# Another load order, narrower first products and new ranks in a planned attention kernel

## The chip, the core and the metric

The kernel runs on one core of a Trainium2 chip. The metric is device microseconds from the start to the end of one execution. Before the change the median of three runs is 588.07 us (587.85 to 589.9). Engines are called as the profile calls them: PE multiplies, PEld loads its weights, DVE, ACT and POOL are the elementwise engines, SP issues DMAs.

## What is computed

Two cross attentions with 8 heads over x (2 x 2048 x 640), all in float32, and an output projection. The first attends from x to 124 text tokens. The second is an adapter over 4 more tokens, whose own queries attend to x before; its result has only 384 different rows, which are gathered to 2048 by fixed indices.

```python
query = hidden_states @ Wq
hs = _mha(query, enc @ Wk, enc @ Wv)                     # 8 heads of 80
ca_q1 = jnp.einsum('btc,th->bch', ca, Wq_ca)[:, indices, :]
ca_hs1 = _mha(ca_q1, residual, residual)                 # residual is x
ca_hs2 = _mha(ca_hs1 @ Wq, ca @ Wk_ca, ca @ Wv_ca)
out = (hs + ca_hs2) @ Wout + b_out + residual
```

## The kernel before

The order of all instructions is made while the program is built. Generators (`x_first`, `queries`, `text_scores`, `chain` and so on) yield pieces of work, `Do(engine, function, after, needs, ...)`, and the class `Desk` plays them against a model of the chip: each piece has a modelled length, each DMA a modelled landing, and every engine's list is written in the order in which the model runs it. On the chip every engine then keeps that order and waits on semaphores, whatever the real times are.

At each step `Desk.run` (L164) looks, engine by engine, for the earliest moment at which a piece could start, and takes among those that are ready then the one with the smallest sum of `order` (the rank given in the code plus an entry of the table `RANKS`, by the generator's name and how many of that name were begun before it) and `change` (L141). `change` is only counted for pieces that say in what shape they use PE's array: nothing in the shape of the moment, `LEAVE` when PE leaves the whole 128x128 array, `SWITCH` when it goes back to it, `ANOTHER` between two smaller shapes. Scores (`sc`, 64-row halves), hidden states (`ph`, 32-column quarters) and all products with Wq and Wout (`pq`, `po`, whole) carry a shape; the adapter's pieces (`s`, `acc`, `pyz`) carry none and have the lowest ranks.

```python
        if mode is None or mode == self.mode:
            return 0.0
        return self.LEAVE if self.mode == self.WHOLE else self.SWITCH if mode == self.WHOLE else self.ANOTHER
```

PE's other filler is `idle_work` (L564): 14 products of zeros (tile `unread`, two passes each), rank 9, that the planner puts wherever it sees PE with nothing else.

The start runs so. `first_loads` (L465) issues on SP: x's rows 0 to 127 and 128 to 255 (`x_rows`, 320 KB each), Wq in five chunks of its 640 rows (`chunk`, the fifth in `last`; the heads' 80 features are regrouped into chunks of 128), x's rows 256 to 511, then the small inputs, Wk_ca and Wk. `x_first` (L624) turns the first 512 rows of x so that features lie on partitions: for each 128 rows (k) DVE first collects the features that are not contiguous (`between`, tile `first_rows`, five copies), PE transposes chunk by chunk (tile `pt_x`), ACT or DVE copies the result into the tile `xt` and marks `("xpart", half, part)`. `queries` with `first=True` (L1160) multiplies by Wq over 256 rows at a time, the first half (k = 0, 1) chunk by chunk of the contraction as Wq lands, the second half later. A product over n rows in float32 is two passes of n columns on PE, for each of two banks and two output chunks.

After that come the keys and values, seven more blocks of 512 rows of x (`x_load`, `queries_fast`, by a scheme with fewer products), the adapter's maximum pass (`s`, reduced by DVE into `mx`), its exponentials (`s` to ACT's `ea`) and contraction (`acc`), for each of two batches, and for each 128 rows the scores, softmax (`m`, `p`, `eb`), a store and reload that turns the probabilities (`kept`, `pT`), the hidden states and the product with Wout, added to x by DVE (`x_more`, `last_rows`).

Of the kernel before, what the change touches and what calls it, by code (L numbers as in the profile page):

```python
# [14 lines left out]
P = 128  # L15
# [49 lines left out]
class Desk:  # L65
# [3 lines left out]
    ENGINES = ("PE", "ACT", "DVE", "POOL", "SP", "NONE")  # L69
    WHOLE, SWITCH, LEAVE, ANOTHER = (P, P), 157.7, 5.4, 131.2  # L70
    START = {(P, P): 0.107, (64, P): 0.143, (P, 64): 0.107, (64, 32): 0.1, (P, 32): 0.03}
# [13 lines left out]
    RANKS = {  # L85
        "adapter": {0: 3, 1: 5.5},
        "chain": {2: 9, 4: -18, 5: 11, 6: -3, 8: -1, 10: -8, 11: -0.6, 19: -3, 24: -3, 25: 8, 30: 11, 32: 8,
            34: -10, 35: -1, 36: -1.3, 39: 2, 41: 3.5, 42: 4, 45: 6, 48: -4, 49: -15, 52: -1, 53: 6, 58: 8,
            60: -6, 61: -6, 62: -9, 64: -1, 72: -3, 80: 2, 85: 3, 87: 7},
        "contract": {0: 5.5, 1: 6, 2: 6, 3: 8},  # L90
        "halves_away": {1: -13, 2: -2, 6: 7},
        "keys": {0: -11},
        "probabilities": {0: 6.1, 8: 9, 9: 6, 11: -7, 14: -3, 15: 4},
        "queries_fast": {0: 4, 4: -3},
        "rest_back": {1: 13, 4: 5, 9: 7, 10: 8},
        "second": {0: 6},
        "softmax": {0: 6, 2: -2, 4: -5, 8: 5, 10: 4, 11: -4, 14: -4, 16: 2, 17: 7, 21: 12, 22: 10, 25: 4},
        "sums_of_wq": {0: 9},
        "text_scores": {0: -3, 1: 9, 12: 5},
        "values_weights": {0: -17},  # L100
        "x_load": {1: 5.1, 4: 7, 5: 6},
        "y_rows": {2: 4, 3: 15, 5: -2},
        "yz_block": {2: 12, 3: -2, 6: 10, 7: 1.3},
    }
# [155 lines left out]
def kernel(  # L260
# [204 lines left out]
    def first_loads():  # L465
# [31 lines left out]
        for k in (0, 1):  # L497
            yield x_rows(k)
        for c in range(4):
            yield chunk(c)  # L500
# [123 lines left out]
    def x_first():  # L624
# [7 lines left out]
        for k in range(4):  # L632
# [4 lines left out]
            )), 1)  # L637
        for h in range(2):
            k0 = 2 * h
            for n, part in enumerate((  # L640
                [(k0, c) for c in range(4)], [(k0 + 1, c) for c in range(4)], [(k0, 4), (k0 + 1, 4)],
            )):

                def turn(s, part=part, n=n, k0=k0):
                    pt = early_bank(s[0], f"pt_x_{k0}_{n}")
                    for i, (k, c) in enumerate(part):
                        transpose(pt[:, i * P : (i + 1) * P], rows_by_chunk(rows_of[0][:, k], last[k], c), ident)
                    return pt

                op = yield Do("PE", turn, [("xlast", k0 + min(n, 1))], needs=[(early, 1)])  # L650
                to = xt[0, 0][0][:, k0 + n, :4] if n < 2 else xt[0, 0][0][:, k0 : k0 + 2, 4]
                src = op.value[:, : len(part) * P].rearrange("p (c s) -> p c s", s=P)
                yield Fork(one(Do(
                    EITHER, lambda to=to, src=src: copy(to, src), [op.at], frees=[(early, op.slots[0][0])],
                    marks=[("xpart", h, n)],
                )), 1)
        yield Do(
            "NONE", lambda: None, [("xpart", h, n) for h in range(2) for n in range(3)],
            frees=[(first_rows, at) for at in rooms] + [(staging, 0)], marks=[("x", 0, 0)],
# [500 lines left out]
    def queries(n, after, first=False):  # L1160
# [8 lines left out]
        if first:  # L1169
            yield Do("NONE", room, [], needs=[(qslots, 1)])  # L1170
            q = q_of[n][0]

            def product(to, h, i, c, start):
                matmul(
                    to, wq_of(i, c), t[:, 2 * h : 2 * h + 2, i, :], start=start, stop=(i == NCH - 1),
                    skip_group_check=True,
                )

            def two(pq, j, h, i):
                for m in range(2):  # L1180
                    product(pq[:, 2 * P * m : 2 * P * (m + 1)], h, i, 2 * j + m, i == 0 and m == 0)

# [8 lines left out]
            for i in range(NCH):  # L1191
                op = yield Do(
                    "PE", lambda i=i: [two(pq[j], j, 0, i) for j in range(2)],
                    [("wq", i)] + [("xpart", 0, k) for k in range(3 if i == NCH - 1 else 2)],
                )
            for j in range(2):
                yield kept(pq[j], j, 0, three[j], op.at)
            for h in range(2):
                for j in range(2 if h else 0):

                    def part(s, j=j):
                        to = bank(s[0], f"pq_{n}_{j}_1")
                        for i in range(2):
                            two(to, j, 1, i)
                        return to

                    op = yield Do("PE", part, after, needs=[(banks, 1)], mode=(P, P))
                    to, s = op.value, op.slots[0][0]
                    for i0, i1 in ((2, 4), (4, NCH)):
                        op = yield Do("PE", lambda i0=i0, i1=i1: [two(to, j, 1, i) for i in range(i0, i1)], mode=(P, P))  # L1210
                    yield kept(to, j, 1, s, op.at)
                for i0, i1 in ((0, 3), (3, NCH)):

                    def fifth(i0=i0, i1=i1, h=h):
                        for i in range(i0, i1):
                            product(pq[2][:, 2 * P * h : 2 * P * (h + 1)], h, i, 4, i == 0 and h == 0)

# [1154 lines left out]
```

## Time and profile before

| | before |
|---|---|
| median of three runs | 588.07 us (587.85 to 589.9) |
| the profiled execution, its time | 588.11 us |
| its span, first to last instruction | 586.4 us |
| PE busy | 578.6 us |
| DVE busy | 392.0 us |
| ACT busy | 313.2 us |
| granted TensorE clock | 0.999 |

The span is shorter than the time of the same execution by 1.7 us, which lie before the first and after the last instruction. In a timeline a row is one or several like instructions of one engine: start, length, engine, line, operation, tiles, shape, count, and in brackets how long the engine stood idle before it and what ended that. Matmuls overlap, so a row's length is longer than the distance to the next row's start; distances of starts are used where a price is wanted. Where a helper records each operation (L208, L218, L233, L253), the line says nothing and the tile's name tells what the instruction is for.

### The profile page before, as it was taken

The numbers are of one execution on the slowest core, as the hardware profiler recorded it, in microseconds if no ns is written. First come the engines' busy times: TensorE is split into PE (matmuls) and PEld (weight loads), VectorE is DVE, ScalarE is ACT, GpSimd is POOL, SyncE is SP. The second block draws the span as 40 slices with busy tenths as digits, with TensorE's granted clock in tenths as the row PEclk, the third lists the DMA queues.
The fourth block names the chain that finished last, engine by engine and source line by source line (L and its number), as shares of the span: only waits on it lengthen the run. The fifth ranks groups of instructions, "written<-read, shape, count | busy, mean of one in ns | idle before, by whom it ended". The sixth has DMA issues, their size and how long they took to land.

```text
span 586.4 us, 12250 instructions
## 1 busy us (share of the span) xinstructions
PE 578.6 (99%) x4681; PEld 374.8 (64%) x4681; DVE 392.0 (67%) x646; ACT 313.2 (53%) x881; POOL 141.7 (24%) x200
## 2 busy tenths in 40 slices
PE   9999999999999999999999999999999999999997
PEld 8786446676766566566576656655556566676675
DVE  2546899999999566356999999853255353544443
ACT  1413276686558789679847626368678612102200
POOL 9102112112205214010115225122041221322342
PEclk9999999999999999999999999999999999999999
DMA  8996876899566967324999959994658577699967
GB/s 254 231 215 116 204 105 180 173 212 182 148 198 149 219 144 193 114 75 155 246 264 260 235 150 206 295 265 122 154 124 248 128 198 201 142 261 267 264 162 195
DMA packets 153012, 112.27 MB, mean 191 GB/s; under 512 B 83701, under 2 KB 126581, under 8 KB 152954
## 3 DMA queue, kind: packets, MB, share of 16 engines
q1 hardware_dynamic: 147322, 100.80, 66.5%
q0 software_dynamic: 5632, 10.69, 10.5%
q8 instruction: 37, 0.61, 0.4%
q14 instruction: 21, 0.17, 0.1%
HBM read 71.23 MB, written 40.22 MB: 190 GB/s over the span
## 4 chain that ended last, share of the span: by engine, by line
PE 85%; DVE 9%; DMA 2%; issue 2%; ACT 2%; DVEq 0%
PE po L208 27%; PE pq L208 23%; PE acc L208 7%; PE ph L208 7%; PE sc L208 6%; PE s L208 6%; DVE mx L233 4%; PE pyz L208 2%; DVE eb L233 1%; PE pv L208 1%; PE pk L208 1%; DMA kept<-eb 1%; DMA zb<-z 1%; DVE m L233 1%; PE unread L208 1%
## 5 line engine op out<-in xcount | busy, mean ns | idle before, releaser
L233 DVE TENSOR_REDUCE mx<-s 128x4 f32<-128x2048 f32 x48 | 109.3, 2276 | 2.4 <-PE s L208 2.4
L233 ACT ACTIVATE ea<-s 128x2048 f32<-128x2048 f32 x48 | 91.0, 1895 | 30.8 <-PE s L208 30.6
L233 ACT ACTIVATE p<-sc,m 128x124 f32<-128x124 f32 x256 | 89.8, 383 | 7.5 <-DVE m L233 6.8
L208 PE MATMUL pq<-xt,wq_sb 128*128 128x256 f32 (+1 forms) x312 | 86.2, 416 | 0.1
L208 PE MATMUL po<-wout_sums,hs 128*128 128x320 f32 x256 | 78.9, 440 | 0.5 <-DVE x_more L233 0.5
L208 PE MATMUL po<-wout_sb,hs 128*128 128x320 f32 x248 | 76.6, 439 | 0.0
L233 DVE TENSOR_TENSOR x_more<-x_more,po 128x320 f32<-128x320 f32 x76 | 36.5, 484 | 52.3 <-PE po L208 51.8
L208 PEld LDWEIGHTS pq<-xt,wq_sb 128*128 128x128 f32 x312 | 56.8, 190 | 21.3 <-issue 13.7
L208 PEld LDWEIGHTS po<-wout_sums,hs 128*128 128x128 f32 x256 | 47.2, 190 | 23.6 <-issue 4.7
L208 PEld LDWEIGHTS po<-wout_sb,hs 128*128 128x128 f32 x248 | 45.6, 190 | 22.8 <-issue 4.2
L233 ACT ACTIVATION_READ_ACCUMULATOR p<-sc,m 128x1 f32 x256 | 57.9, 226 | 0.0
L2107 POOL DMA_INDIRECT x_more<-o,query x19 | 29.4, 1550 | 101.2 <-DVE x_more L233 86.5
L208 PE MATMUL acc<-ea,y_sb 128*32 128x384 f32 (+2 forms) x768 | 51.2, 385 | 0.0
L233 DVE TENSOR_REDUCE m<-sc 128x4 f32<-128x496 f32 x64 | 40.0, 662 | 11.2 <-PE sc L208 11.1
L233 DVE TENSOR_TENSOR last_rows<-last_rows,po 128x320 f32<-128x320 f32 x52 | 25.0, 485 | 31.6 <-PE po L208 31.2
L233 ACT COPY hs<-ph 128x512 f32<-128x512 f32 (+1 forms) x34 | 18.3, 545 | 51.7 <-PE ph L208 51.7
L208 PE MATMUL ph<-pT,vpad 128*32 128x256 f32 x768 | 45.0, 381 | 0.0
L233 ACT ACTIVATE p<-p,r 128x124 f32<-128x124 f32 x120 | 36.3, 387 | 10.9 <-DVE r L233 10.9
L233 POOL TENSOR_TENSOR p<-p,r 128x992 f32<-128x992 f32 x8 | 14.8, 1853 | 112.8 <-DVE r L233 112.8
L233 DVE STREAM_TRANSPOSE eb<-p 128x1024 f32<-128x1024 f32 x32 | 39.4, 1232 | 1.9 <-DMA kept<-eb 1.1
L208 PE MATMUL pq<-xt,wq 128*128 128x512 f32 (+1 forms) x90 | 40.1, 564 | 0.0
L208 PEld LDWEIGHTS sc<-kmain,q 64*128 64x128 f32 x512 | 31.5, 187 | 11.4 <-issue 6.1
(212 smaller groups left out, 814.7 us busy)
## 6 DMA issues: line engine op xcount, KB each, us to landing
kept<-eb SPq DMA_DIRECT2D x32, 512.0 KB, 4.4
pT<-kept SPq DMA_DIRECT2D x64, 256.0 KB, 6.7
landing<-away SPq DMA_DIRECT2D x60, 128.0 KB, 3.6
xi<-in_x_dram SPq DMA_DIRECT2D x56, 128.0 KB, 3.9
x_more<-in_x_dram SPq DMA_DIRECT2D x19, 320.0 KB, 6.6
out_dram<-x_more SPq DMA_DIRECT2D x18, 320.0 KB, 4.9
last_rows<-in_x_dram SPq DMA_DIRECT2D x13, 320.0 KB, 5.5
y<-yt SPq DMA_DIRECT2D x16, 256.0 KB, 3.5
```

What stands on the lines that cost most here:

```text
L208: self.pin(self.nc.tensor.matmul(out, lhsT, rhs, **kw))
L233: self.pin(getattr(engine, what)(*args, **kw))
L2107: desk.pin(nc.gpsimd.indirect_dma_start(out=t, out_offset=None, in_=o2_of[b], in_offset=bass.IndirectOffsetOnAxis(ap=query[:, st : st + 1] ...
```

## The change

- `first_loads`: Wq's chunk 0 is issued between x's first and second rows, chunk 1 behind the second rows; all else follows as before.
- `x_first`: the first 256 rows are turned in other groups, for each 128 rows features of chunks 0 and 1 together (these need no copies by `between`), then chunks 2, 3 and 4. Rows 256 to 511 keep four chunks together and a shared fifth. The marks are now per 128 rows.
- `queries`, first: the products with chunk 0 of the contraction run over 128 rows, once for each k; the other chunks over 256 as before.
- `Desk`: SWITCH, LEAVE, ANOTHER and all of RANKS have other values.

```diff
--- before.py
+++ after.py
@@ -67,7 +67,7 @@
 
 
     ENGINES = ("PE", "ACT", "DVE", "POOL", "SP", "NONE")
-    WHOLE, SWITCH, LEAVE, ANOTHER = (P, P), 157.7, 5.4, 131.2
+    WHOLE, SWITCH, LEAVE, ANOTHER = (P, P), 328.5, 9.9, 185.7
     START = {(P, P): 0.107, (64, P): 0.143, (P, 64): 0.107, (64, 32): 0.1, (P, 32): 0.03}
     DRAIN = {
         ((P, P), (32, P)): 0.136, ((P, P), (64, P)): 0.035, ((P, P), (P, 64)): 0.056, ((P, P), (P, 32)): 0.067,
@@ -83,24 +83,26 @@
 
 
     RANKS = {
-        "adapter": {0: 3, 1: 5.5},
-        "chain": {2: 9, 4: -18, 5: 11, 6: -3, 8: -1, 10: -8, 11: -0.6, 19: -3, 24: -3, 25: 8, 30: 11, 32: 8,
-            34: -10, 35: -1, 36: -1.3, 39: 2, 41: 3.5, 42: 4, 45: 6, 48: -4, 49: -15, 52: -1, 53: 6, 58: 8,
-            60: -6, 61: -6, 62: -9, 64: -1, 72: -3, 80: 2, 85: 3, 87: 7},
-        "contract": {0: 5.5, 1: 6, 2: 6, 3: 8},
-        "halves_away": {1: -13, 2: -2, 6: 7},
-        "keys": {0: -11},
-        "probabilities": {0: 6.1, 8: 9, 9: 6, 11: -7, 14: -3, 15: 4},
-        "queries_fast": {0: 4, 4: -3},
-        "rest_back": {1: 13, 4: 5, 9: 7, 10: 8},
-        "second": {0: 6},
-        "softmax": {0: 6, 2: -2, 4: -5, 8: 5, 10: 4, 11: -4, 14: -4, 16: 2, 17: 7, 21: 12, 22: 10, 25: 4},
-        "sums_of_wq": {0: 9},
-        "text_scores": {0: -3, 1: 9, 12: 5},
-        "values_weights": {0: -17},
-        "x_load": {1: 5.1, 4: 7, 5: 6},
-        "y_rows": {2: 4, 3: 15, 5: -2},
-        "yz_block": {2: 12, 3: -2, 6: 10, 7: 1.3},
+        "adapter": {0: 1, 1: 2},
+        "chain": {2: 8, 4: -11, 5: 7, 6: -2, 8: -11, 11: -4, 14: 11, 15: 16, 19: -14, 24: -4, 25: 3, 30: 3.1,
+            32: 4, 34: 10, 36: 2, 41: 0.5, 42: 1, 43: 0.5, 44: -10, 45: -10, 48: -8, 50: -5, 51: -5, 52: 7,
+            54: 10, 55: 10, 56: 10, 68: -4, 76: -3, 81: 2, 86: 2, 87: 3},
+        "contract": {0: 5, 1: 4.5, 2: 8, 3: 8},
+        "halves_away": {1: -4, 2: -2, 4: 4, 6: 6},
+        "keys": {0: -10},
+        "probabilities": {3: -8, 5: -4, 8: 12, 9: -3, 10: -2, 12: 6, 13: 6, 15: 7},
+        "queries_fast": {0: 5, 3: 4},
+        "rest_back": {1: 11, 4: 5, 7: 8, 9: 9, 10: 5, 14: 2},
+        "second": {0: 2.3},
+        "softmax": {0: 5, 2: -7, 3: 6.2, 4: -4, 7: -11, 8: 2, 10: -5, 12: -20, 14: -3, 17: 9, 20: -2, 21: 7,
+            22: 7, 25: -5, 29: 2, 30: 6},
+        "sums_of_wq": {0: 5.7},
+        "text_scores": {0: -8, 1: 3.4, 12: 9},
+        "values_weights": {0: -18},
+        "x_load": {1: 4.2, 4: 5},
+        "y_rows": {2: 2, 3: 6, 4: 4},
+        "y_weights": {0: 1},
+        "yz_block": {2: 16, 5: 3.5, 6: 5},
     }
 
     def __init__(self, tc):
@@ -496,7 +498,8 @@
 
         for k in (0, 1):
             yield x_rows(k)
-        for c in range(4):
+            yield chunk(k)
+        for c in (2, 3):
             yield chunk(c)
         yield Do("SP", last, [], marks=[("wq", 4)])
         for k in (2, 3):
@@ -635,11 +638,13 @@
                 lambda k=k: between(last[k], rows_of[0][:, k, :]),
                 [("xrows", k)], marks=[("xlast", k)], rank=1,
             )), 1)
-        for h in range(2):
-            k0 = 2 * h
+        for k0 in range(4):
+            whole = [(k0, c) for c in range(4)]
             for n, part in enumerate((
-                [(k0, c) for c in range(4)], [(k0 + 1, c) for c in range(4)], [(k0, 4), (k0 + 1, 4)],
+                [whole[:2], whole[2:] + [(k0, 4)]] if k0 < 2 else [whole, [(2, 4), (3, 4)][: 2 * (k0 - 2)]]
             )):
+                if not part:
+                    continue
 
                 def turn(s, part=part, n=n, k0=k0):
                     pt = early_bank(s[0], f"pt_x_{k0}_{n}")
@@ -647,15 +652,18 @@
                         transpose(pt[:, i * P : (i + 1) * P], rows_by_chunk(rows_of[0][:, k], last[k], c), ident)
                     return pt
 
-                op = yield Do("PE", turn, [("xlast", k0 + min(n, 1))], needs=[(early, 1)])
-                to = xt[0, 0][0][:, k0 + n, :4] if n < 2 else xt[0, 0][0][:, k0 : k0 + 2, 4]
+                op = yield Do("PE", turn, [("xrows" if k0 < 2 and n == 0 else "xlast", k0)], needs=[(early, 1)])
+                if k0 == 3 and n:
+                    to = xt[0, 0][0][:, 2:4, 4]
+                else:
+                    to = xt[0, 0][0][:, k0, part[0][1] : part[-1][1] + 1]
                 src = op.value[:, : len(part) * P].rearrange("p (c s) -> p c s", s=P)
                 yield Fork(one(Do(
                     EITHER, lambda to=to, src=src: copy(to, src), [op.at], frees=[(early, op.slots[0][0])],
-                    marks=[("xpart", h, n)],
+                    marks=[("xpart", k0, n)],
                 )), 1)
         yield Do(
-            "NONE", lambda: None, [("xpart", h, n) for h in range(2) for n in range(3)],
+            "NONE", lambda: None, [("xpart", k, n) for k in range(4) for n in range(2) if k != 2 or n == 0],
             frees=[(first_rows, at) for at in rooms] + [(staging, 0)], marks=[("x", 0, 0)],
         )
 
@@ -1170,15 +1178,15 @@
             yield Do("NONE", room, [], needs=[(qslots, 1)])
             q = q_of[n][0]
 
-            def product(to, h, i, c, start):
-                matmul(
-                    to, wq_of(i, c), t[:, 2 * h : 2 * h + 2, i, :], start=start, stop=(i == NCH - 1),
-                    skip_group_check=True,
-                )
-
-            def two(pq, j, h, i):
+            def product(to, k, i, c, start):
+                matmul(to, wq_of(i, c), t[:, k, i, :], start=start, stop=(i == NCH - 1), skip_group_check=True)
+
+            def two(pq, j, k, i):
                 for m in range(2):
-                    product(pq[:, 2 * P * m : 2 * P * (m + 1)], h, i, 2 * j + m, i == 0 and m == 0)
+                    at = 2 * P * m + (P if k == 1 else 0)
+                    rows = k if isinstance(k, int) else slice(*k)
+                    n = P if isinstance(k, int) else 2 * P
+                    product(pq[:, at : at + n], rows, i, 2 * j + m, i == 0 and m == 0 and k != 1)
 
             def kept(pq, j, h, s, at):
                 return Fork(one(evacuate(
@@ -1189,10 +1197,11 @@
             op = yield Do("NONE", lambda s: [bank(i, f"pq_{n}_{c}") for c, i in enumerate(s)], [], needs=[(banks, 3)])
             pq, three = op.value, op.slots[0]
             for i in range(NCH):
-                op = yield Do(
-                    "PE", lambda i=i: [two(pq[j], j, 0, i) for j in range(2)],
-                    [("wq", i)] + [("xpart", 0, k) for k in range(3 if i == NCH - 1 else 2)],
-                )
+                for k in (0, 1) if i == 0 else ((0, 2),):
+                    op = yield Do(
+                        "PE", lambda i=i, k=k: [two(pq[j], j, k, i) for j in range(2)],
+                        [("wq", i), *([("xpart", k, 0)] if i == 0 else [("xpart", k, int(i > 1)) for k in range(2)])],
+                    )
             for j in range(2):
                 yield kept(pq[j], j, 0, three[j], op.at)
             for h in range(2):
@@ -1201,19 +1210,21 @@
                     def part(s, j=j):
                         to = bank(s[0], f"pq_{n}_{j}_1")
                         for i in range(2):
-                            two(to, j, 1, i)
+                            two(to, j, (2, 4), i)
                         return to
 
                     op = yield Do("PE", part, after, needs=[(banks, 1)], mode=(P, P))
                     to, s = op.value, op.slots[0][0]
                     for i0, i1 in ((2, 4), (4, NCH)):
-                        op = yield Do("PE", lambda i0=i0, i1=i1: [two(to, j, 1, i) for i in range(i0, i1)], mode=(P, P))
+                        op = yield Do("PE", lambda i0=i0, i1=i1: [two(to, j, (2, 4), i) for i in range(i0, i1)], mode=(P, P))
                     yield kept(to, j, 1, s, op.at)
                 for i0, i1 in ((0, 3), (3, NCH)):
 
                     def fifth(i0=i0, i1=i1, h=h):
                         for i in range(i0, i1):
-                            product(pq[2][:, 2 * P * h : 2 * P * (h + 1)], h, i, 4, i == 0 and h == 0)
+                            product(
+                                pq[2][:, 2 * P * h : 2 * P * (h + 1)], slice(2 * h, 2 * h + 2), i, 4, i == 0 and h == 0
+                            )
 
                     op = yield Do("PE", fifth, ["wq4", *(after if h else [])], mode=(P, P))
             yield Fork(first_halves(pq[2], three[2], op.at), 0)
```

## The prediction

> **What bounds the kernel now.** I read the page first: busy shares, the slices, the chain.
>
> ```profile
> span 586.4 us, 12250 instructions
> PE 578.6 (99%) x4681; PEld 374.8 (64%) x4681; DVE 392.0 (67%) x646; ACT 313.2 (53%) x881; POOL 141.7 (24%) x200
> PE   9999999999999999999999999999999999999997
> PE 85%; DVE 9%; DMA 2%; issue 2%; ACT 2%; DVEq 0%
> ```
>
> PE has work in every slice, and 85% of the chain that ended last is PE. The diff takes no multiplication away, so time can only come out of what PE does besides streaming: its waits, its fillers, its changes between the whole array and parts of it, and its start. The list of who waited for whom, PE alone, comes next:
>
> ```profile
> PE unread L208 <- DVE zeros L233: 1.1, 1, 1.1
> PE pm L218 <- ACT p L233: 0.7, 1, 0.7
> PE s L208 <- DVE mx L233: 0.6, 1, 0.6
> PE pt_x L218 <- DVE first_rows L233: 0.5, 1, 0.5
> PE po L208 <- DVE x_more L233: 0.5, 1, 0.5
> PE pt_acc L218 <- ACT accs L233: 0.2, 1, 0.2
> PE s L208 <- ACT ea L233: 0.2, 1, 0.2
> ```
>
> After the start (first and fourth row) the waits are 0.7 + 0.6 + 0.5 + 0.2 + 0.2 = 2.2 us in all. The reader is to see how small that is: 2.2 of 586.4.
>
> **The start, before.** The timeline of the first 22 us, with the hand-over times of the first DMAs from the view of DMA issues (one narrow window each; the last number is us from issue to landing):
>
> ```profile
> 0.81 0.87 SPq L253 DMA_DIRECT2D xz<-in_x_dram  x2
> xz<-in_x_dram SPq DMA_DIRECT2D x1, 320.0 KB, 2.8
> 1.72 6.78 SPq L253 DMA_DIRECT2D wq_sb<-in_L_xattn_Wq_dram  x11
> wq_sb<-in_L_xattn_Wq_dram SPq DMA_DIRECT2D x1, 320.0 KB, 5.4
> 1.12 3.78 PE L208 MATMUL unread<-zeros 128*128 128x128 f32 x16 [1.12 <-DVE zeros L233]
> 5.67 1.03 ACT L233 COPY xt<-pt_x 128x512 f32<-128x512 f32 x2 [3.58 <-PE pt_x L218]
> 6.11 0.69 DVE L233 COPY xt<-pt_x 128x512 f32<-128x512 f32 x1 [0.43 <-PE pt_x L218]
> 6.13 1.06 PE L208 MATMUL unread<-zeros 128*128 128x128 f32 x8
> 7.02 8.80 PE L208 MATMUL pq<-xt,wq_sb 128*128 128x256 f32 x40
> L208 PEld LDWEIGHTS pq<-xt,wq_sb 128*128 128x128 f32 x312 | 56.8, 190 | 21.3 <-issue 13.7
> 5.00:10.00 5.00, 5.00 (x32) 4.67 (x31) 1.34 (x6) 0.96 (x2) 4.68 (x19) 1.00 1.00 259
> ```
>
> x's first rows land at 0.81 + 2.8 = 3.6 us. The second chunk of Wq is the fourth transfer; it is issued behind the first chunk, at 2.2 by the 0.43 to 0.48 an issue takes here (0.87 for two, then 1.72), and lands at 2.2 + 5.4 = 7.6. At 259 GB/s a piece of 320 KB (0.328 MB) takes 1.27 us, so the third transfer lands near 6.3 and the second near 5.0 by the rate. PE starts the first products at 7.02, when the second rows' transpose has been copied out (DVE, 6.11 + 0.69 = 6.80); from 6.13 to then it multiplies zeros. A pass over 256 rows comes every (8.80 - 0.38) / 39 = 0.216 us (0.38 being what one instruction lasts), one over 128 rows every (1.06 - 0.28) / 7 = 0.111; at the very start, in the first 16, every (3.78 - 0.42) / 15 = 0.224. (0.28 and 0.42 are likewise one instruction's own length, an estimate from the merged rows; an error of 0.05 in them changes nothing below.) Each chunk takes 8 such passes, so the second chunk's products begin at 7.02 + 8 x 0.216 = 8.75.
>
> **The change at the start.** Three DMAs swap places: Wq's chunk 0 is issued second, x's second rows third; the number of issues on SP is the same and everything behind them keeps its place. Chunk 0 then comes near 5.0 and the second rows near 6.3. The first rows are turned as chunks 0, 1 straight from the loaded rows, without DVE's copies between, then chunks 2 to 4. Transposes of x stay 20. The products of chunk 0 become 16 passes over 128 rows in place of 8 over 256: 16 x 0.111 - 8 x 0.216 = +0.05 us. The evacuations of a row's transposes become 256 and 384 columns wide where they were 512 and half of 256; they run on ACT and DVE, idle here (3.58 us before ACT's first copy).
>
> Best case: chunk 1's products start when it lands, 7.6, and not 8.75: -1.1 us. Worst case: the order on PE is fixed when the program is built, by modelled landings that are later than the real ones, and its fillers are part of that order. The second rows now come one transfer later, their first two transposes and a copy stand ahead of chunk 0's second half, then 8 passes (0.9): landing 6.3, transposes 2 x 0.111, copy and hand-over 0.7 (the DVE copy's row), passes 0.9 give 8.1, and with fillers in between 8.7: nothing won. Nor is a loss excluded: if PE still takes 0.224 a pass, the first rows' eight passes fit before the second rows' copy is out at 6.3 + 0.2 + 0.7 = 7.2, but the second rows' end at 7.2 + 8 x 0.224 = 9.0, with a filler (two passes of 0.111) between at 9.2: +0.4 is the other end. I take -0.4, nearer to the worst than the best case because fillers have filled every gap of the plan before.
>
> Whether it lasts depends on the next link:
>
> ```profile
> 12.97 0.67 DVE L233 COPY first_rows<-xz 128x64 f32<-128x64 f32 x5
> 15.86 0.69 DVE L233 COPY q<-pq 128x512 f32<-128x512 f32 x1 [2.22 <-PE pq L208]
> 16.47 2.01 DVE L233 COPY first_rows<-xz 128x64 f32<-128x64 f32 x5
> 16.62 1.43 POOL L233 MEMSET vpad<- 128x768 f32 x2
> 18.29 0.44 PE L218 MATMUL pt_x<-ident,first_rows 128*128 128x128 f32 x2 [0.52 <-DVE first_rows L233]
> 21.44 0.39 PE L208 MATMUL unread<-zeros 128*128 128x128 f32 x2
> 21.77 0.39 PE L208 MATMUL unread<-zeros 128*128 128x128 f32 x2
> ```
>
> DVE's five copies for the fourth rows take 2.01 here where the same five took 0.67; POOL clears vpad in exactly that stretch. PE waits 0.52 for them. If the products end 0.4 earlier, the copies begin at 16.1 and still meet the clearing, and the 0.4 is lost there; if they end over 0.7 earlier, they are through before 16.62, and the wait goes. Fillers at 21.44 to 22.2 (two of 0.2) are the only slack after it. So for this link and the fillers: -0.9 at best, 0 or a lost 0.4 at worst; I take -0.4. **Start in sum: -0.8, ends +0.4 and -2.0.**
>
> **The other ranks and constants.** Every rank is new, so the order of PE's remaining 550 us is. No row of before shows the new order; I bound it. Waits: the 2.2 us above are the most that can go; as much again could come; I take half of them, -1.1, since which op waited is an accident of one order and the new one has the same buffers. Array changes: the timeline of PE shows their price.
>
> ```profile
> 149.73 1.99 PE L208 MATMUL pq<-xt,wq_sb 128*128 128x256 f32 x8
> 151.65 1.16 PE L208 MATMUL sc<-kmain,q 64*128 64x124 f32 x16
> 153.14 2.00 PE L208 MATMUL pq<-x_sums,wq_sums 128*128 128x256 f32 x8
> 156.47 1.89 PE L208 MATMUL pq<-xt,wq_sums 128*128 128x256 f32 x8
> 158.29 0.50 PE L208 MATMUL s<-zop,cop 32*128 32x512 f32 x4
> 163.44 0.50 PE L208 MATMUL s<-zop,cop 32*128 32x512 f32 x4
> 163.88 1.16 PE L208 MATMUL sc<-kmain,q 64*128 64x124 f32 x16
> L208 PE MATMUL sc<-kmain,q 64*128 64x124 f32 x512 | 37.7, 285 | 0.0
> ```
>
> Eight passes between two excursions take 151.65 - 149.73 = 1.92 us; eight that follow whole-array work and precede an excursion 158.29 - 156.47 = 1.82; eight in a row 8 x 0.216 = 1.73. So leaving costs 0.09, coming back 0.10: 0.2 us an excursion. There are 512 / 16 = 32 score blocks (sc). The one at 151.65 leaves the whole array by itself, the one at 163.88 rides behind an s block. If half do as the first, 16 could be joined to another excursion. LEAVE goes from 5.4 to 9.9, so a planner in whole mode holds a score block back behind products up to 9.9 ranks worse (before 5.4); and the gap between SWITCH and ANOTHER goes from 26.5 to 142.8, so once outside it takes another part-array op ahead of returning whatever the ranks. Both push towards joining. Seven of the 16 joined: -1.4; ends -3.2 (all) and +2.0 (ten more excursions, by ranks that split them). A score block held back costs its softmax a later start, and behind it on SP the store and reload of its probabilities; that is the slow rival.
>
> Sum against the profiled execution's own 588.1 (span 586.4 and 1.7 around it; the median of the runs is the same): 588.1 - 0.8 - 1.1 - 1.4 = **584.8**.
>
> **Rivals.**
> *Everything fits.* Start -2.0, waits -2.2, joins -2.6 (13 blocks): 581.3. For it: each is there to be taken. Against: the three must come true together.
>
> *The start is given back and the ranks are neutral.* The copies meet the clearing, or fillers eat it: 588.1 - 0.5 = 587.6. This is also the case that the change does not do what it says: the second rows, one transfer later, hold the products until 8.7.
>
> *DVE becomes the bound between 60 and 180 us.*
>
> ```profile
> 60.00:180.00 120.00, 119.23 (x788) 75.13 (x788) 116.77 (x149) 77.69 (x291) 17.97 (x15) 1.00 0.76 171
> L233 DVE TENSOR_REDUCE m<-sc 128x4 f32<-128x496 f32 x64 | 40.0, 662 | 11.2 <-PE sc L208 11.1
> L233 DVE STREAM_TRANSPOSE eb<-p 128x1024 f32<-128x1024 f32 x32 | 39.4, 1232 | 1.9 <-DMA kept<-eb 1.1
> ```
>
> DVE is busy 116.77 of 120 us there. One score block more in that stretch brings DVE 2 x 0.662 + 1.232 = 2.55 us. The spare 3.2 hold one; from the second on, PE's s blocks wait for mx, unless products are ready. Three more cost 7.65 - 3.2 = 4.4 us, and if nothing else is won than the start, 588.1 - 0.8 + 4.4 = 591.7: slower. For it: new ranks move softmaxes by up to ten places. Against: the adapter's s blocks (rank 0) still come first, and queries are in reserve.
>
> *The split products' weight loads are not hidden.* Sixteen loads of 190 ns (PEld pq) that do not overlap would add 16 x 0.19 = 3.0 to the forecast: 587.8. Against it: the fillers are passes over 128 rows with a load each, and 8 of them took 1.06 together, 0.111 each. The Trainium skill, "TensorE: Matmul & The Clock Gate", section "The mechanism", says a load overlaps running products only where its row group differs, which never holds for the whole array; by that rule this rival is what happens. The trace disagrees with it, 0.111 and 0.216 a pass with a load each.
>
> **How the numbers follow.** Chances: forecast 0.44, its own range 583.2 to 586.4 (about three quarters of it under 585.1); everything fits 0.20; start given back 0.11; DVE 0.22; weight loads 0.03. A measurement of this kernel tells 0.5%, 2.9 us, from no change: under 585.1 is faster, over 591.0 slower. Faster 0.32 + 0.20 = 0.52; same 0.12 + 0.11 + 0.03 = 0.26; slower 0.22 (the case with two blocks or fewer is put to the forecast's upper edge). Range: half of the fits-all case and half of the DVE case stay inside: 580.8 to 592.
>
> **What would show it.** Start: the first pq row begins near 5 to 6, with 128 columns, and chunk 1's before 8.7. Link: the five copies for the fourth rows take 0.7 or 2.0, PE's wait for first_rows is gone or not. Waits: the list of PE's waits adds up to about 1 us after the start. Joins: fewer sc rows between two pq or po rows. DVE rival: a wait of PE for mx, m or eb of over 1 us between 60 and 180. The prediction is wrong if PE's waits after the start exceed 3 us or if excursions are more than before.

## The result, and the profile after

The changed kernel takes 587.67 us (median of 20 runs, 586.46 to 589.32), the kernel before 588.79 on the same chips (20 runs, 587.85 to 590.88). The ratio of the times is 0.9977, with its 95% interval [0.9967, 0.9986]: 1.1 us less by the medians, 1.4 by the ratio. The forecast of 584.8 had 3.3 us less. A second measurement further down gives 0.999 [0.998, 0.9999], by its medians 0.5 us less. So the change does something, in the direction forecast, and between about a sixth and two fifths of the forecast size.

The page of the kernel after, its head and its chain:

```profile
span 586.0 us, 12251 instructions
PE 578.4 (99%) x4689; PEld 374.5 (64%) x4689; DVE 392.7 (67%) x645; ACT 309.1 (53%) x869; POOL 141.0 (24%) x200
PE 79%; DVE 9%; DMA 6%; ACT 4%; issue 2%; SPq 0%; DVEq 0%; ACTq 0%
```

PE is busy as long as before (578.4 against 578.6) with eight matmuls more, the split products. The profiled execution took 587.72 us, span 586.0: 0.4 less than before's. PE's own waits, from the list of who waited for whom (engine, tile, line, releaser; us in total, times, longest):

```profile
PE unread L210 <- DVE zeros L235: 1.1, 1, 1.1
PE po L210 <- DVE x_more L235: 0.8, 1, 0.8
PE pq L210 <- DVE mt L235: 0.6, 1, 0.6
PE s L210 <- ACT ea L235: 0.4, 2, 0.3
PE s L210 <- DVE mx L235: 0.4, 1, 0.4
PE pt_acc L220 <- ACT accs L235: 0.2, 1, 0.2
```

Behind the start they add up to 0.8 + 0.6 + 0.4 + 0.4 + 0.2 = 2.4 us, where it was 2.2. The wait for `first_rows` is gone and so is that of `pm`; one for `mt` has come and that for `x_more` has grown. Behind the start nothing was won in this list; the 0.5 of `first_rows` belongs to the start, and the experiments tell what took it away. A second profile of the same kernel, further down, has 0.6 + 0.4 + 0.4 + 0.2 + 0.2 = 1.8 us there, so the list differs by some tenths from one execution to the next.

The start on PE's timeline:

```profile
5.47 1.06 PE L210 MATMUL pq<-xt,wq_sb 128*128 128x128 f32 x8
6.37 0.39 PE L210 MATMUL unread<-zeros 128*128 128x128 f32 x2
6.73 0.44 PE L220 MATMUL pt_x<-ident,xz 128*128 128x128 f32 x2
7.01 0.39 PE L210 MATMUL unread<-zeros 128*128 128x128 f32 x2
7.26 0.52 PE L220 MATMUL pt_x<-ident,first_rows 128*128 128x128 f32 x3
7.61 0.61 PE L210 MATMUL unread<-zeros 128*128 128x128 f32 x4
8.06 7.97 PE L210 MATMUL pq<-xt,wq_sb 128*128 128x128 f32 x40
15.86 0.38 PE L220 MATMUL pt_x<-ident,xz 128*128 128x128 f32 x2
```

and DVE's of the same execution:

```profile
6.71 0.65 DVE L235 COPY first_rows<-xz 128x64 f32<-128x64 f32 x5 [1.68 <-DMA xz<-in_x_dram]
16.67 1.46 DVE L235 COPY first_rows<-xz 128x64 f32<-128x64 f32 x5
```

The first products start at 5.47 instead of 7.02, over 128 columns. But x's second rows land only just before 6.71, so that their eight passes start at 8.06 and chunk 1's at 8.06 + 8 x 0.111 = 8.95, where it was 8.75; the first products end 0.2 us later than before (15.86 against 7.02 + 40 x 0.216 = 15.66). The 1.5 us won at the front have turned into eight passes over zeros and into transposes that wait for the load.

In the stretch from 60 to 180 us, where DVE was the rival bound (columns: stretch, its length, then busy us and instructions of PE, PEld, DVE, ACT, POOL, clock, DMA share, GB/s):

```profile
60.00:180.00 120.00, 119.98 (x791) 75.83 (x791) 114.90 (x149) 77.66 (x291) 18.45 (x16) 1.00 0.74 166
```

DVE is busy 114.90, less than the 116.77 of before. That rival did not come.

### The profile page after: what moved, and what is told of

It reads as the page before. It is cut to its first block, busy times and chain, and to the rows that moved or that the text cites. A ratio compares the mean times of both kernels' runs of the same rounds, so it can differ in the third digit from the quotient of the medians.

```text
span 586.0 us, 12251 instructions
## 1 busy us (share of the span) xinstructions
PE 578.4 (99%) x4689; PEld 374.5 (64%) x4689; DVE 392.7 (67%) x645; ACT 309.1 (53%) x869; POOL 141.0 (24%) x200
## 4 chain that ended last, share of the span: by engine, by line
PE 79%; DVE 9%; DMA 6%; ACT 4%; issue 2%; SPq 0%; DVEq 0%; ACTq 0%
PE po L210 26%; PE pq L210 23%; PE ph L210 6%; PE acc L210 6%; PE sc L210 5%; PE s L210 5%; DVE mx L235 3%; DMA pT<-kept 2%; PE pyz L210 2%; DMA kept<-eb 2%; ACT ea L235 2%; ACT p L235 1%; DMA x_more<-in_x_dram 1%; PE pv L210 1%; PE pk L210 1%
## 5 line engine op out<-in xcount | busy, mean ns | idle before, releaser
L210 PE MATMUL pq<-xt,wq_sb 128*128 128x256 f32 (+2 forms) x320 | 86.3, 410 | 0.6 <-DVE mt L235 0.6
L210 PE MATMUL po<-wout_sb,hs 128*128 128x320 f32 x240 | 74.6, 439 | 0.8 <-DVE x_more L235 0.8
L235 DVE TENSOR_TENSOR x_more<-x_more,po 128x320 f32<-128x320 f32 x72 | 34.4, 483 | 46.9 <-PE po L210 46.4
L210 PEld LDWEIGHTS po<-wout_sb,hs 128*128 128x128 f32 x240 | 44.2, 190 | 22.7 <-issue 2.3
L2118 POOL DMA_INDIRECT x_more<-o,query x18 | 27.9, 1550 | 126.9 <-DVE x_more L235 109.2
L235 DVE TENSOR_TENSOR last_rows<-last_rows,po 128x320 f32<-128x320 f32 x56 | 26.8, 482 | 29.0 <-PE po L210 27.3
L235 ACT CAST rests<-landing 128x512 fp32r<-128x512 f32 x30 | 18.8, 635 | 37.4 <-PE sc L210 19.1
```

Source lines behind the costliest of these rows:

```text
L210: self.pin(self.nc.tensor.matmul(out, lhsT, rhs, **kw))
L235: self.pin(getattr(engine, what)(*args, **kw))
L2118: desk.pin(nc.gpsimd.indirect_dma_start(out=t, out_offset=None, in_=o2_of[b], in_offset=bass.IndirectOffsetOnAxis(ap=query[:, st : st + 1] ...
```

## The experiments

The planner's order can be written down as a list of pieces and replayed, so that a kernel keeps one start and takes the other kernel's order behind x's first block; and excursions (runs of PE's work in smaller shapes between two pieces that use the whole array) are counted in PE's list of instructions: 96 before, 93 after. The ratios are to the kernel before, measured beside each run, with 95% intervals.

**The start and the order, each alone.**

```diff
+LATER = (
+    "74bd7422N240c7922N530b49b4N5fe643bbN45987e1e..."
...
     def run(self):
+        names = [int(LATER[i : i + 8], 16) for i in range(0, len(LATER), 9)]
...
+            if not self.known(("x", 0, 0)):
+                self.issue(*self.chosen())
+                continue
```

The changed start with before's order:

> The changed start (load order, narrower first products, transposes in other groups), and behind x's first block every engine's list in the order of the kernel before. Theory A (the prediction's: the start is worth 0.4 to 0.8 us on its own, and the ranks the rest): 0.4 to 0.8 us less than before, ratio 0.9986 to 0.9993. Rival B (the start gives nothing, since the second rows come one transfer later and the fillers fill the gap; first products end at 15.9 us where they ended at 15.7): ratio 0.9995 to 1.0005. Rival C (the start is the whole of the measured gain, the ranks nothing): ratio 0.9977, 1.3 us less.

589.22 us against 588.43, ratio 1.0007 [0.9991, 1.0023]: no gain, as rival B had it; if anything it is later. The old start with the order of after:

> The start of the kernel before, and behind x's first block every engine's list in the order that the changed ranks and constants make. Theory A: what the start leaves of the measured 1.3 us, so 0.5 to 0.9 us less than before, ratio 0.9985 to 0.9991. Rival B: all of it, ratio 0.9977. Rival C: ratio 0.9995 to 1.0005. By the count of excursions from the whole array in the two lists of PE (96 before, 93 here) at 0.2 us each it would be 0.6 us less.

587.7 us, ratio 0.9986 [0.9968, 1.0004]. So far as these two runs tell, what the change wins lies in the order; the interval still takes in no gain at all, that of the second measurement, which comes next, does not.

**The kernel after and that partner, once more, on one chip.**

> The kernel after once more, beside the run of the old start with its order behind, on the same chip: what the changed start is worth, and a second profile of its loads. Theory A (with the new load order some packets of the first loads stall): the second rows land at 6.4 or later again, chunk 1 at 8.2 or later, and the time is within 0.5 us of that of the old start with the same order. Theory B (chance): the second rows land before 6.0, chunk 1's products begin within 0.2 us of 8.5 at the earliest the fillers leave, and the time is 0.4 us or more under that run.

> The old start with the order of the kernel after behind it, once more, as the partner of the kernel after on the same chip, and for a second profile of the loads in the old order. Theory A: third transfer near 5.9, chunk 1 near 7.6, no packet between 3 and 6 us that takes over 1.2 us; 587.7 us, ratio to before 0.9986. Theory B (stalls come by chance in either order): a third transfer at 6.5 or later here.

587.77 us and 587.65 us; against before 0.999 [0.998, 0.9999] and 0.999 [0.9981, 0.9999]. The whole changed start is worth 0.1 us of loss here, nothing that can be told. In both profiles of the kernel after, and in that of the changed start with before's order, the second rows came late. DVE's rows show it, in the second profile of the kernel after:

```profile
7.13 0.64 DVE L235 COPY first_rows<-xz 128x64 f32<-128x64 f32 x5 [2.16 <-DMA xz<-in_x_dram]
```

and in that of the changed start with before's order:

```profile
7.96 0.64 DVE L468 COPY first_rows<-xz 128x64 f32<-128x64 f32 x5 [2.92 <-DMA xz<-in_x_dram]
```

The copies start when the last of the transfer's 16 semaphore steps has come; a table of these landings stands further down.

**The two halves of the new start, each with the order of after.** Only the loads swapped:

```diff
         for k in (0, 1):
             yield x_rows(k)
-        for c in range(4):
+            yield chunk(k)
+        for c in (2, 3):
             yield chunk(c)
```

> The kernel before with one change at the start, Wq's first chunk loaded ahead of x's second rows; products over 256 rows and x's transposes as before; behind x's first block the order of the kernel after. Compared with the run that has the start of before and the same order behind (587.7 us, x's second rows there by 4.6, the third transfer by 5.9, chunk 1 by 7.6). Theory A (the load order itself makes the second rows late): the second rows land at 6.5 or later, some of their 16 parts well behind the rest, chunk 1 lands at 8.4 or later, and the last turn of x is 0.5 to 1.3 us later, 588.2 to 589.0 us. Theory B (the late landings came with the narrower products, or by chance): the third transfer lands near 5.9 and chunk 1 near 7.6, as in the three executions with the old load order, and the time is within 0.3 us of 587.7.

589.0 us, ratio 1.001 [1.0001, 1.0019], against 0.9986 and 0.999 of the old start with the same order: 1.2 to 1.4 us slower. Theory A held: the second rows landed at 7.7. On PE's timeline:

```profile
5.15 1.50 PE L446 MATMUL unread<-zeros 128*128 128x128 f32 x12
7.75 0.44 PE L456 MATMUL pt_x<-ident,xz 128*128 128x128 f32 x2 [1.10 <-DMA xz<-in_x_dram]
8.18 0.66 PE L456 MATMUL pt_x<-ident,first_rows 128*128 128x128 f32 x4
9.29 7.17 PE L446 MATMUL pq<-xt,wq_sb 128*128 128x256 f32 x32 [0.46 <-ACT xt L471]
```

With products over 256 rows all of PE's work stands behind the second rows: it waits 1.10 us for them and begins at 9.29. The other half, narrow products with the old load order, is the diff above the other way round, in the kernel after:

> The other half of the changed start alone: products of chunk 0 over 128 rows and x turned by pairs of features, but the loads in the order of before (x's first rows, x's second rows, chunk 0); behind x's first block the order of the kernel after. Theory A (the load order is what costs): chunk 0 lands at 5.9, chunk 1 at 7.6, the products of chunk 1 begin between 7.7 and 8.4 instead of 8.9, and the time is 0.4 to 1.0 us under the 587.7 us of the run with the old start and the same order behind. Rival (the narrow products cost what they win, by their extra passes or by weight loads that aren't hidden): chunk 1's products begin at 8.9 or later and the time is 587.7 or more; eight passes over 128 rows would then take over 1.2 us instead of 1.06.

587.4 us, ratio 0.9988 [0.9979, 0.9996]: the same as the old start with the same order. Chunk 1's products began at 8.44, as theory A had it, and the sixteen narrow passes from 6.65 to then took 0.112 each, so the rival's reason is out; but in the profiled execution the five copies for the fourth rows then fell on POOL's clearing (below), PE waited 0.6 for them, and the gain was gone at this link. So neither half wins: the narrow products only repair what the load order costs.

**The fillers.** In the kernel after and in the one just described, no filler behind the first six:

```diff
-    FAST, SPARE, IDLE = 2, 0, 14
+    FAST, SPARE, IDLE = 2, 0, 6
```

> The kernel after with the fillers behind the first six taken out, all else alike. Theory A (fillers hold chunk 1's products back): these begin near 8.5 instead of 8.95 and the last turn of x is 0.3 to 0.5 us earlier; 587.3 us. Theory B (chunk 1's landing holds them back): they begin right behind that landing, at 8.4 or later, PE waits for it where the fillers were, and the time is within 0.2 us of that of the kernel after, 587.7.

> The kernel of the narrow-products run, with the fillers (products over zeros that nothing reads) that the planner puts between the first products taken out behind the first six. Theory A (fillers in front of work that is ready cost what the early products win): chunk 1's products begin 0.3 to 0.6 us earlier than in the narrow-products run, and so does the last turn of x; 586.7 to 587.3 us. Rival (PE waits there for loads, and the fillers only fill the waits): no more than 0.2 us of difference, and a wait of PE for a DMA or for xt where the fillers stood.

586.83 us, 0.9979 [0.997, 0.9988], and 587.72 us, 0.9992 [0.9979, 1.0005]. The profile of the first, PE:

```profile
5.25 1.06 PE L446 MATMUL pq<-xt,wq_sb 128*128 128x128 f32 x8
7.25 0.44 PE L456 MATMUL pt_x<-ident,xz 128*128 128x128 f32 x2 [0.94 <-DMA xz<-in_x_dram]
7.78 0.52 PE L456 MATMUL pt_x<-ident,first_rows 128*128 128x128 f32 x3
8.15 8.07 PE L446 MATMUL pq<-xt,wq_sb 128*128 128x128 f32 x40
```

The fillers had only filled a wait for the loads: without them PE waits 0.94 for the second rows, and chunk 1's products begin at 9.15, not at 8.5. In the other kernel PE waited 1.4 for chunk 0, which landed at 7.21 there. So it is a landing that sets the start, not the fillers (the second rows', where theory B had named chunk 1's). The 586.83 us are less than either theory gave, and no profile here says why. The kernel after was not run on that chip; the ratio 0.9979 lies between the two of the kernel after, 0.9977 and 0.999. No kernel of this study is shown to beat it.

**The clearing of `vpad`.** POOL clears it between its small loads of `ca` instead of behind them:

```diff
         for row in range(0, P, T):
             if row % G < MAX:
+                if b == 0 and row == 2 * G:
+                    for i in range(B):
+                        desk.g_memset(vpad[i], 0.0)
                 desk.g_dma_start(
...
-            "POOL", lambda: [desk.g_memset(vpad[b], 0.0) for b in range(B)], [], marks=["vpad"]
+            "POOL", lambda: None, [], marks=["vpad"]
```

> The changed kernel, all lists the same, but POOL clears vpad between its eighth and ninth small DMA and not behind the sixteenth, so at 11 to 13 us in place of 16.3 to 17.7. Theory (the clearing holds up DVE's five copies for the fourth rows): these take 0.7 us and not 1.46, PE's start on the fourth rows' last transposes comes 0.2 to 0.4 us earlier, and the time falls by up to 0.3 us against the changed kernel (ratio to before 0.9972). Rival (the copies are long for another reason, as bank or DMA traffic): they stay at 1.4 us or more and the ratio stays 0.9977.

587.74 us, 0.9983 [0.9965, 1.0001]: no gain that can be told. Its profile is of the slowest of its twelve runs (589.35 us), and the second rows landed at 7.78 there, which hides the rest. What the profiles do show is the price itself. Old start with the order of after, second profile (POOL, then DVE):

```profile
15.62 1.43 POOL L471 MEMSET vpad<- 128x768 f32 x2
```

```profile
17.05 0.63 DVE L471 COPY first_rows<-xz 128x64 f32<-128x64 f32 x5
```

The narrow products with the old load order:

```profile
16.81 1.43 POOL L471 MEMSET vpad<- 128x768 f32 x2
```

```profile
16.15 2.16 DVE L471 COPY first_rows<-xz 128x64 f32<-128x64 f32 x5
```

With the clearing moved to 10.85 the copies take 0.63, as the theory had it. Clear of the clearing the five mostly take 0.63 to 0.67; where they meet it, it is 2.16, 2.01 (before), 1.46 (after) or, in the second profile of the kernel after, where they begin 1.05 us into it, 0.80. They are not slowed evenly: in the kernel before the shortest copy and the median one take 0.16 us, the longest takes 1.67. In all ten profiles where copies meet the clearing, those that are under way end 0.04 to 0.19 us behind its end, so DVE is held up until POOL is through, on a tile that DVE does not touch. Whether they meet depends on when POOL's sixteen small loads are done, 15.4 to 16.9 in these executions. The clearing is not the only thing that can hold the copies: with the changed start and before's order two of the five for the third rows took 0.79 and 0.73, and ended at 16.2, when POOL was still issuing its small loads.

**The constants alone, the table alone.** The kernel before with either half of the planner's new numbers:

```diff
-    WHOLE, SWITCH, LEAVE, ANOTHER = (P, P), 157.7, 5.4, 131.2
+    WHOLE, SWITCH, LEAVE, ANOTHER = (P, P), 328.5, 9.9, 185.7
```

> The kernel before with the three constants SWITCH, LEAVE, ANOTHER of the change alone; the table of ranks and the start are as before. The prediction's reason (the constants push towards joining part-array work into fewer excursions): 1 us less or better, ratio 0.998 or less. Rival (the planner's list for PE now has 105 excursions where it had 96, so at 0.2 us each they cost 1.8 us, and ranks that were fitted to the old constants no longer fit): 1.8 us more or worse, ratio 1.003 or more, with new waits of PE.

611.28 us, ratio 1.0381 [1.0338, 1.0424]: the prediction's reason is out, and the rival's 1.8 us has the direction, far too small. And with the new RANKS but the old three constants:

> The kernel before with the table of ranks of the change alone: SWITCH, LEAVE and ANOTHER stay as they were, and so does the start. The order of PE's work has 103 excursions out of the whole array, before 96, after 93. Theory A (ranks and constants only fit together, and a misfit costs in waits rather than in excursions): 595 us or more; PE's waits behind the start add up to 8 us or more, while seven more excursions at 0.2 us make no more than 1.4 us of it. Rival (the table carries what the change wins, and the constants alone were a bad case): 587 to 590 us, waits under 4 us.

613.42 us, ratio 1.0444 [1.0422, 1.0467]. Each half alone makes the kernel 23 to 25 us slower; only together they win 0.7. The excursions are 105 and 103. With the table alone PE's waits behind the start add up to 21.1 us, as theory A had it. PE's waits with the constants alone:

```profile
PE s L208 <- DVE mx L233: 4.4, 5, 2.1
PE ph L208 <- issue: 3.1, 1, 3.1
PE pyz L208 <- DVE xt L233: 2.8, 1, 2.8
PE s L208 <- ACT ea L233: 1.5, 1, 1.5
PE pq L208 <- DVE q L233: 1.4, 2, 1.1
PE po L208 <- DVE x_more L233: 1.2, 2, 0.6
```

All of them behind the start add up to 15.9 us, 13.7 more than before. Nine more excursions at 0.2 are 1.8. The span is 22.7 longer, and the rest has another place, which the run with the table alone shows best. PE's timeline, and the stretches around it:

```profile
158.15 0.80 PE L210 MATMUL s<-zop,cop 32*128 32x512 f32 x4 [4.07 <-DVE mx L235]
160.32 3.78 PE L210 MATMUL pq<-xt,wq_sb 128*128 128x256 f32 x8 [1.37 <-ACT p L235]
164.03 0.80 PE L210 MATMUL s<-zop,cop 32*128 32x512 f32 x4
164.76 2.04 PE L210 MATMUL pq<-x_sums,wq_sb 128*128 128x256 f32 x8
```

```profile
150.00:155.00 5.00, 4.08 (x56) 3.33 (x54) 5.00 (x8) 1.24 (x2) 0.66 (x1) 1.00 0.24 82
155.00:160.00 5.00, 0.80 (x4) 0.29 (x4) 5.00 (x7) 1.23 (x7) 4.31 (x4) 0.80 0.71 156
160.00:165.00 5.00, 4.68 (x13) 3.06 (x14) 3.49 (x5) 4.42 (x26) 1.84 (x1) 0.51 0.98 174
165.00:170.00 5.00, 5.00 (x40) 4.06 (x40) 4.97 (x5) 1.17 (x2) 1.51 (x1) 1.00 1.00 139
```

PE waits 4.07 us for a maximum of DVE's; then the granted clock (the figure of 0.51 in the stretch from 160 to 165) is half, eight passes take 3.78 where the next eight take 2.04, and four of `s` 0.80 instead of 0.50. The Trainium skill, "TensorE: Matmul & The Clock Gate", section "What's actually happening", says that PE's clock falls to half after an idle window of about 3.4 us; this row agrees. Other rows do not: with the constants alone the granted clock is 0.5 behind waits of 2.77, 1.47 and 3.05 us (from 187.2, 279.3 and 576.3 us on), and with the table alone it stays at 1.00 behind one of 3.48 (at 572.6). So in this case shorter waits can bring the half clock too, and a long one need not. With the mean clock of 0.989 against 0.999, the constants' run loses about 0.010 x 609 = 6 us this way (an estimate): 13.7 + 1.8 + 6 = 21.5 of its 22.7.

**The price of an excursion.** In the order of after, eight places where a score block and a block of `s` follow each other are split by the product behind them; as a list of PE's work at one of them:

```diff
 sc<-kmain,q x16
 sc<-krest,rests x8
-s<-zop,cop x4
 pq<-x_sums,wq_sums x8
+s<-zop,cop x4
 pq<-xt,wq_sb x4
```

> The kernel after with eight joined excursions split: where a score block (sc) and a block of s follow each other, the product that comes behind the two is put between them; all else is in the order of after. 101 excursions instead of 93. Prediction's price (0.2 us an excursion): 1.6 us more than the kernel after, 589.3 us, with no new wait of PE over 0.5 us. Rival (leaving and returning mostly lie hidden, or the price is another for sc than for s): within 0.5 us of the kernel after. A third way: the eight s blocks, one product later each, make ACT and the product of their sums late, and PE's waits for ea, mx or mt grow by over 1 us.

593.32 us, ratio 1.0085 [1.0072, 1.0098], 5.6 us over the kernel after on the same chip. At that place, the kernel after:

```profile
120.89 1.16 PE L210 MATMUL sc<-kmain,q 64*128 64x124 f32 x16
122.38 0.50 PE L210 MATMUL s<-zop,cop 32*128 32x512 f32 x4
122.81 1.99 PE L210 MATMUL pq<-x_sums,wq_sums 128*128 128x256 f32 x8
127.33 1.95 PE L210 MATMUL pyz<-xt,wyz 64*32 64x512 f32 x32
```

and split:

```profile
121.38 1.16 PE L446 MATMUL sc<-kmain,q 64*128 64x124 f32 x16
122.87 1.99 PE L446 MATMUL pq<-x_sums,wq_sums 128*128 128x256 f32 x8
124.79 0.51 PE L446 MATMUL s<-zop,cop 32*128 32x512 f32 x4
128.02 2.21 PE L446 MATMUL pyz<-xt,wyz 64*32 64x512 f32 x32
```

From the first row to the last it is 6.44 us there and 6.64 here, for the same work: the 0.20 of the prediction. But eight of them are 1.6, and the span grew by 591.1 - 585.8 = 5.3. The rest is mostly waits:

```profile
PE s L446 <- DVE mx L471: 3.5, 6, 0.8
```

That is 3.1 more than in the kernel after. An `s` block that comes one product later gives DVE its maximum later, and the next `s` block, at its old place, waits for it. So the third way of the expectation is what mostly happened. Whether PE's array changes cost 0.2 is a small matter beside whether the adapter's blocks are in time.

## Why the prediction was wrong in size

**Start (forecast -0.8, measured 0).** The term failed at its landing: "Chunk 0 then comes near 5.0 and the second rows near 6.3" was worked out from the rate, and every figure behind it stands on that. Chunk 0 did come (4.75), the second rows did not (6.69 in the same profile). The landings, with the longest packet that began between 3 and 6 us:

| kernel | third transfer lands at, us | longest packet, us |
|---|---|---|
| new load order: after, twice | 6.69, 7.11 | 1.47, 1.22 |
| changed start, before's order | 7.93 | 1.30 |
| only the loads swapped | 7.71 | 1.28 |
| after, `vpad` earlier; no fillers; split | 7.78; 7.21; 6.72 | 1.17; 1.57; 1.13 |
| old load order: before; with the order of after, twice | 5.90; 5.94, 5.94 | 0.59; 0.97, 1.06 |
| constants alone; table alone | 6.21; 6.45 | 1.10; 0.84 |
| narrow products; without fillers too | 5.42; 7.21 | 0.73; 1.29 |

In all seven executions with the new order the third transfer, x's second rows, lands at 6.69 or later; with the old order it does so once in seven. The parts of the transfer do not come late together: in the kernel after 14 of the 16 are there by 5.88, the last two at 6.47 and 6.69. A packet of 1.1 to 1.6 us that begins at 3.9 to 4.6 us, where most take about 0.1, goes with it each time, and chunk 1 follows late (8.41 against 7.57). That the stalled packet holds the late parts back is argued from the times, not shown: two executions with packets of 1.06 and 1.10 landed in time. This was the rival "that the change does not do what it says", with the reason that it gave (second rows one transfer later) and a delay that it did not know. Why packets stall, and why mostly in this order, stays open; nothing was tried on it. The link was right: the copies do stretch when they meet the clearing, and its 0.5 us wait of PE is gone in the kernel after; but it is gone with the old start and the new order too (copies of 0.65 and 0.63), so it is not the start's gain.

**Waits (forecast -1.1, measured +0.2 to -0.4).** "I take half of them" had no row behind it. The list is 2.2 us before; with the order of after it is 2.4 and 1.8 in the two profiles of the kernel after, 1.9 and 1.8 in those with the old start. Other waits came for those that went. At 0.4% of the span the order of before had as little slack to give as the order of after.

**Joins (forecast -1.4, by count and price -0.6).** The price held (0.20), the number did not: three excursions fewer by the count, instead of seven. Two steps fell. "16 could be joined" counted score blocks that lead their excursion, but most of these have an `s` block right behind them and are joined already: excursions that hold a score block and no `s` block are 5 in the trace before and 5 in that after. There were five to join, not 16, and their number did not change. The other step is "Both push towards joining". Score blocks that leave the whole array with no `s` block ahead of them are 13 before and 15 after. The constants alone make 105 excursions out of 96, and 10 with a score block and no `s` block. So a constant of a greedy planner says little by itself. With a larger LEAVE a block may be held back and then miss the `s` block that it could have ridden with; that is argued, the planner's choices were not followed one by one. An excursion also had a cost outside the term: an `s` block moved is paid in waits for `mx`, 3.1 us for eight.

**What held.** The direction; the first products at 5.47 over 128 columns; no cost for the split products (0.111 a pass, with a weight load each, so that rival is out); DVE with room to spare; no wait of PE over 0.8 us behind the start. Added up, 0 for the start, +0.2 to -0.4 for the waits and -0.6 for the joins make 0.4 to 1.0 us less, where 0.5 to 1.4 was measured. The rival "the start is given back and the ranks are neutral", 587.6, has nearly the measured number, by luck and for other reasons: the start gave nothing, and the order gave 0.6 to 0.8 (ratios 0.9986 and 0.999). How that divides between joins and the copies that no longer meet the clearing is too small for these runs to tell.

## What to carry to other kernels

When PE is busy 99% of the span and waits 2 us of 586, a list of waits that short is the remainder of a fit, not a store to take half from; here new ranks won some tenths. Before counting work that could be joined, count what is joined already. Numbers that were fitted together are one change: here each half cost 23 to 25 us and both together won 0.7, so do not infer a constant's effect from the rule in which it stands. And where a start hangs on which transfer comes first, take the time of the last of its parts from traces of several executions, since the mean rate says nothing of one packet that stalls.

## What was not expected of the hardware

- A wait of PE of 4.07 us was followed by a stretch at a granted clock of 0.51; the eight passes behind it took 3.78 us instead of 2.04, and two `s` blocks 0.80 instead of 0.50 each. The wait was followed by some 2.3 us more (an estimate, 1.74 + 2 x 0.30). Waits of 1.47 to 3.05 us were followed by the half clock as well, one of 3.48 was not.
- DVE's five copies took 0.63 to 0.67 us, or up to 2.16 where they met POOL's clearing of a tile that they do not touch; the copies under way ended within 0.2 us behind the clearing's end.
- In 8 of 14 executions one to four of a transfer's 16 parts came up to 2.4 us behind the others, each time with one or two 2,560-byte packets of 1.1 to 1.6 us, the longest of which began between 3.9 and 4.6 us from the start.
